# A two-layer graph attention kernel: the preparation of its first layer reordered, with projections in four column tiles, x loaded ahead of the stores, and the last targets spread by TensorE

## The chip, the cores and the metric

The kernel runs on one core of a Trainium2 chip. The core has five engines that work side by side, each through its own instructions in order: TensorE (PE, with its weight loads shown apart as PEld), VectorE (DVE), ScalarE (ACT), GpSimd (POOL) and SyncE (SP). SP issues all the transfers of this kernel; they then run on sixteen DMA engines. On-chip memory (SBUF) and the accumulators of TensorE (PSUM) have 128 partitions each. The metric is the device time of one execution in microseconds (us). "Before" took 4940.27 us, the median of three runs (4938.2 to 4942.55).

## What is computed

x is 4096 x 512, adj is 4096 x 4096, all in fp32. Each of two layers normalises x, applies a relu, and adds an attention over the graph with 8 heads of 64 columns. The change lies in the first layer alone:

```python
h = relu(layernorm(x))
data1 = (h @ W.T + b).reshape(N, 8, 64)
src = einsum('nhd,hd->nh', data1, src_proj)
trg = einsum('nhd,hd->nh', data1, trg_proj)
e = leaky(src.T[:, :, None] + trg.T[:, None, :])      # slope 0.01; [head, row, column]
scores = softmax(e + adj, axis=-1)
x = x + concat_over_heads(scores @ data1[head])
```

The second layer (projections to keys, queries and values, masked softmax, projection back) follows and is left as it is.

## The kernel before, in words

**The order** is written out by hand: inside `tc.manual_schedule()` the instructions stand on every engine in the order in which the Python code emits them. Pools of buffers and the dependencies between tiles add the waits. A tile of a pool with n buffers waits until the readers of the tile n allocations earlier are done. The transfers of SP use eight completion semaphores in turn, so a transfer also waits, on SP, for the one eight before it.

**The preparation of layer 0** works on eight blocks of 512 rows (`XR` = 4 tiles of 128 rows, `NQ` = 8). A loop over q (line 446) runs as a pipeline, each iteration doing another stage of several blocks:

- `load_rows` (310): a block of x, 1 MB, into one of the three buffers of pool `pa`. These three buffers later hold the rows of adj.
- `moments` (316) on VectorE, `deviations` (323) on ScalarE, `normed` (327): mean and variance, the square root, then reciprocal and shift on VectorE and the normalised rows `hn` on GpSimd.
- `turned_rows` (342): sixteen 128 x 128 transposes on TensorE (tile `htp`); ScalarE takes them with a relu into `hT`.
- `halves` (357): `lp` = `u`.T applied to `hT`, with the four row tiles of the block side by side in four column tiles of TensorE; VectorE adds the bias `cs` into `lr`. Each quarter of `lr` holds 8 source logits and 8 target logits for 128 rows. Four stores of 4 KB each write the target logits to `trg_d` in HBM.
- `sources` (373): `lr` turned by TensorE (tile `sp`), copied into `src` by VectorE.
- `first_features` (381): data1 for the first pair of heads (tile `mp`), two row tiles at a time; `first_features_out` (395) adds the bias on VectorE. After both halves of a block it also issues the store of that block's `hT`, 1 MB, to `hT_d`.

`u` holds W.T times the two projection vectors of each head, so that source and target logits come straight from `hT`. `prepared` (269), in iteration 1, makes it: VectorE spreads the projection vectors (`col`) into `by_head`, sixteen matmuls with W (`wn`) stationary give `up`, another sixteen give the bias, and VectorE copies both out. `turned_weights` (295) transposes W into `wt`.

**The targets** must stand on all 128 partitions, since the logits of 128 rows against 4096 columns are one ScalarE instruction: `leaky` (145), targets as the input, the row's source as a bias per partition. `load_targets` (123) reads `trg_d` back with a broadcast, in four parts of 1024 columns for each of the two heads, after every second block.

**The main loop** (474) then takes one head of a group of 128 rows at each step s: `leaky`, `masked` (152, VectorE adds a row of adj and takes the row's extreme, in two halves), `exps` (165, ScalarE), transposes on TensorE (`turned`, `taken`), and the product with the features (`weighted`). `hT_d` is read back here, for the features of the next pair of heads. The first three steps also work off what is left of the first features.

Of the kernel before, what the change touches and what calls it, by code (L numbers as in the profile page):

```python
# [8 lines left out]
F32 = mybir.dt.float32  # L9
AF = mybir.ActivationFunctionType  # L10
ALU = mybir.AluOpType
# [4 lines left out]
P = 128  # L16
EPS = 1e-5
SLOPE = 0.01
# [5 lines left out]
def kernel(  # L24
# [74 lines left out]
    with tc.tile_pool(name="a0k", bufs=1) as pk, tc.tile_pool(name="a0v", bufs=4) as pv, tc.tile_pool(  # L99
# [42 lines left out]
            nc.sync.dma_start(a, adj[bass.ts(G.g, P), bass.ts(f, CH)])  # L142
            rows_of_adj[G, f] = a

        def leaky(G, h):
            t = pt.tile([P, N], F32, name="t")
            nc.scalar.activation(  # L147
                t, targets[G.c, h], AF.Prelu, bias=src[:, G.g, 2 * G.c + h : 2 * G.c + h + 1], alpha=SLOPE
            )
            G.t[h] = t  # L150

        def masked(G, h, f):

# [98 lines left out]
        bb = pk.tile([P, HD], F32, name="bb")  # L252
        cs = pk.tile([P, 1], F32, name="cs")

        def load_wn():
            wn = []
            for i in range(2):
                wn.append(pv.tile([P, HC // 2, DM], F32, tag="v", name="wn"))
                nc.sync.dma_start(
                    wn[i], w0[bass.ts(i, HD // 2), :].rearrange("(c p) i -> p c i", p=P)  # L260
                )
            col = psb.tile([P, 3, HC], F32, name="col")
            for i, vec in enumerate(
                (src_proj.rearrange("x h d -> (x h d)"), trg_proj.rearrange("x h d -> (x h d)"), b0)
            ):
                nc.sync.dma_start(col[:, i], vec.rearrange("(c p) -> p c", p=P))
            return wn, col

        def prepared(wn, col):


            by_head = px.tile([P, HC, SQ], F32, tag="att", name="by_head")
            nc.vector.memset(by_head, 0.0)
            for c in range(HC):
                for half in range(2):
                    rows = bass.ts(half, D)
                    at = 2 * c + half
                    nc.vector.tensor_copy(by_head[rows, c, at : at + H + 1 : H], col[rows, 0:2, c])
            up = ptr.tile([P, TW], F32, tag="tr", name="up")
            for kc in range(KC):  # L280
                for c in range(HC):
                    nc.tensor.matmul(
                        up[:, bass.ts(kc, SQ)], lhsT=wn[c // 2][:, c % 2, bass.ts(kc, P)], rhs=by_head[:, c],
                        start=(c == 0), stop=(c == HC - 1),
                    )
            for j in range(NS):
                for c in range(HC):
                    nc.tensor.matmul(
                        up[bass.ts(j, SQ), 512:513], lhsT=by_head[:, c], rhs=col[:, 2, c : c + 1],
                        start=(c == 0), stop=(c == HC - 1),  # L290
                    )
            nc.vector.tensor_copy(u.rearrange("p c k -> p (c k)"), up[:, :P])
            nc.vector.tensor_copy(cs, up[:, 512:513])

        def turned_weights(wn):
            for j in range(KC // 2):
# [60 lines left out]
        def halves(R, q):  # L357

            lp = ptr.tile([P, TW], F32, tag="tr", name="lp")
            for kc in range(KC):  # L360
                for r in range(XR):
                    nc.tensor.matmul(
                        lp[bass.ts(r, SQ), :P], lhsT=u[:, kc], rhs=R.hT[:, r, kc, :],
                        start=(kc == 0), stop=(kc == KC - 1),
                    )
            R.lr = pp.tile([P, TW], F32, tag="pT", name="lr")[:, :P]
            nc.vector.tensor_scalar(R.lr, lp[:, :P], cs, None, ALU.add)
            for r in range(XR):
                nc.sync.dma_start(
                    trg_d[:, bass.ts(q * XR + r, P)], R.lr[r * SQ + H : r * SQ + 2 * H, :]  # L370
                )

        def sources(R, q):

# [20 lines left out]
        def first_features_out(q, j, tp):  # L395
            nc.vector.tensor_add(
                feats[0][q // 2][:, bass.ts(q % 2 * 2 + j, 2), :],
                tp[:, : 2 * PR].rearrange("p (r d) -> p r d", r=2),
                bb[:, :PR].unsqueeze(1).to_broadcast([P, 2, PR]),
            )  # L400
            if j == 1:
                nc.sync.dma_start(
                    hT_d[bass.ts(q, XR)].rearrange("r p k -> p r k"),
                    rows[q].hT.rearrange("p r k n -> p r (k n)"),
                )

        def sources_by_sets():

# [16 lines left out]
        def step(n):  # L425
            return groups[n // 2], n % 2

        with tc.manual_schedule():
            NQ = NB // XR
            TB = 8  # L430
            rows = [load_rows(0)]
            wn, col = load_wn()
            rows.append(load_rows(1))
            nc.sync.dma_start(bb, b0.partition_broadcast(P))
            todo = [(q, j) for q in range(NQ) for j in range(XR // 2)]
            made = []

            def some_features(ready):
                if todo and todo[0][0] < ready:
                    made.append(first_features(*todo.pop(0)))  # L440

            def some_out():
                if made:
                    first_features_out(*made.pop(0))

            for q in range(NQ + 4):
                if q + 2 < NQ:
                    rows.append(load_rows(q + 2))
                some_out()
                if 0 <= q - 2 < NQ:  # L450
                    turned_rows(rows[q - 2], q - 2)
                if 0 <= q - 1 < NQ:
                    normed(rows[q - 1])
                if q < NQ:
                    moments(rows[q])
                    deviations(rows[q])
                if q == 1:
                    prepared(wn, col)
                    turned_weights(wn)
                n = q - 3  # L460
                if 0 <= n < NQ:
                    halves(rows[n], n)
                    if (n + 1) * XR % TB == 0:
                        for h in range(2):
                            load_targets(0, h, n * XR // TB, NB // TB)
                if 0 <= n - 1 < NQ:
                    sources(rows[n - 1], n - 1)
                some_features(q - 2)
            some_out()
            for f in range(NCH):  # L470
                load_adj(groups[0], f)
            leaky(*step(0))
            endings = []
            for s in range(total + 6):
                G, h = step(s) if s < total else (None, 0)
                for half in range(2):

                    if s < total and half == h and s // 2 + 1 < len(groups):
                        load_adj(groups[s // 2 + 1], h)
                    n = 2 * s + half - LEAD  # L480
                    turn = 0 <= n < 2 * total
                    if turn:
                        T, i = groups[n // HALVES], n % HALVES
                        trs = turned(T, i)
                    if s < 3:
                        some_features(NQ)
                        some_features(NQ)
                    if (s, half) == (3, 1):
                        assert not todo and not made
                        sources_by_sets()  # L490
                    if half == 0 and 0 <= s - 1 < total:
                        exps(*step(s - 1))
                    if half == 1 and s + 1 < total:
                        leaky(*step(s + 1))

                        c, at = divmod(s + 3, 2 * NB)
                        if 0 < c < PAIRS and at < 2:
                            load_targets(c, at)
                    if s < total:
                        masked(G, h, half)  # L500
                    if s < 3:
                        some_out()
                        some_out()
                    for e in endings:
                        next(e, None)
                    if turn:
                        taken(T, i, trs)
                    if 1 <= n <= 2 * total:
                        W, w = groups[(n - 1) // HALVES], (n - 1) % HALVES
                        weighted(W, w)  # L510
                        if w == 0:
                            load_rows_turned(W)
                        if W.g == NB - 1 and W.c + 1 < PAIRS:
                            load_feats(W.c + 1, w)
                        if w == HALVES - 1:
                            endings = [*endings[-1:], finish(W)]
# [696 lines left out]
```

## Time and profile before

| What | Value |
|---|---|
| runs | 4938.2, 4940.27, 4942.55 us |
| the profiled execution | 4940.09 us |
| its span | 4938.3 us |
| TensorE busy | 4719.5 us, 96% |
| VectorE busy | 4462.5 us, 90% |
| ScalarE busy | 3857.6 us, 78% |
| GpSimd busy | 459.2 us, 9% |
| transfers | 819.44 MB, 166 GB/s over the span |
| first matmul | 17.08 us |
| first logits (`leaky`) | 88.30 us |
| first exponential (`exps`) | 102.37 us |

The span runs from the first to the last instruction of the profiled execution; the time of a run is a little longer. In the chain of waits each line gives a start, a duration and what the end of the kernel hung on at that moment: a transfer, an instruction of an engine, or the sequencer of one (SPq). In the timeline a line gives start, duration, engine, source line, operation, output, inputs, shapes and how many instructions it stands for. An fp32 matmul makes two passes in the records: 16 instructions are "x32". Idle time of an engine means nothing by itself; what counts is who waits for whom.

### The profile page before, as it was taken

What the parts mean: (1) busy time and instruction counts of PE and PEld (TensorE: products, weight loads), DVE (VectorE), ACT (ScalarE), POOL (GpSimd) and SP (SyncE); (2) the same over time, 40 slices, a digit from 0 to 9 for tenths busy, and PEclk for the clock granted to TensorE, in tenths of its full rate; (3) what the DMA queues carried; (4) which work ended last, traced back from release to release, by engine and by line L of the source; (5) the groups of instructions that cost most, each with busy time, mean ns of one, the idle gap of its engine ahead of it and who ended that gap; (6) DMA issues with size and microseconds to landing.
All of it is one profiled execution on the core that took longest, in us unless ns stands there. A gap on an engine that the chain in (4) does not pass through costs nothing.

```text
span 4938.3 us, 144474 instructions
## 1 busy us (share of the span) xinstructions
PE 4719.5 (96%) x61554; PEld 3518.5 (71%) x61554; DVE 4462.5 (90%) x7841; ACT 3857.6 (78%) x4301; POOL 459.2 (9%) x932
## 2 busy tenths in 40 slices
PE   6999999999999958989989999999999999999998
PEld 5888888888888847767756666666666666666664
DVE  4999999999999898888749999999999999999981
ACT  4999999999999899888748888766666666666660
POOL 2000000000000011111123333100000000000000
PEclk8999999999999979999999999999999999999999
DMA  6444454445444384444367787633445343534435
GB/s 233 158 152 157 162 193 161 152 153 206 153 156 158 115 181 135 143 140 135 111 192 249 241 265 237 223 130 131 152 152 170 130 156 129 189 129 136 158 124 192
DMA packets 358838, 819.44 MB, mean 166 GB/s; under 512 B 60080, under 2 KB 179120, under 8 KB 333104
## 3 DMA queue, kind: packets, MB, share of 16 engines
q1 hardware_dynamic: 358192, 810.21, 50.0%
q8 instruction: 481, 7.88, 0.6%
q14 instruction: 165, 1.35, 0.1%
HBM read 669.26 MB, written 140.77 MB: 164 GB/s over the span
## 4 chain that ended last, share of the span: by engine, by line
PE 57%; ACT 15%; DVE 15%; issue 8%; DMA 3%; SPq 1%; POOL 0%; DVEq 0%; ACTq 0%; POOLq 0%
PE sc L920 20%; PE o L1004 20%; ACT t L168 6%; PE tr L986 5%; DVE t L158 5%; DVE pT L192 4%; ACT t L147 4%; DVE bt L609 3%; PE tr L181 3%; PE o L203 3%; ACT pT L190 2%; PE oo L1087 2%; ACT bt L641 2%; DVE bt L648 2%; DMA ba<-in_adj_dram 1%
## 5 line engine op out<-in xcount | busy, mean ns | idle before, releaser
L936 DVE CUSTOM_DVE_ANT_0 t<-sc,a 128x512 f32<-128x512 f32 x2048 | 1285.7, 683 | 99.3 <-PE sc L920 52.0
L971 ACT ACTIVATE t<-t,nm 128x1024 f32<-128x1024 f32 x1024 | 1165.9, 1142 | 103.1 <-DVE nm L960 103.0
L1004 PEld LDWEIGHTS o<-t,v 128*64 128x64 f32 x16384 | 883.8, 137 | 429.4 <-issue 321.2
L920 PE MATMUL sc<-k,q 64*32 64x512 f32 x16384 | 1028.1, 597 | 10.5 <-DVE nm L936 10.4
L1004 PE MATMUL o<-t,v 128*64 128x128 f32 x16384 | 1007.4, 276 | 0.4 <-ACT oT L1013 0.4
L158 DVE CUSTOM_DVE_ANT_0 t<-t,a 128x2048 f32<-128x2048 f32 x384 | 876.0, 2281 | 41.2 <-ACT t L147 41.0
L978 DVE STREAM_TRANSPOSE t<-t 128x1536 f32<-128x1536 f32 x512 | 908.2, 1774 | 1.1 <-ACT t L971 1.1
L181 PE MATMUL tr<-ident,t 128*128 128x128 f32 x6144 | 781.5, 278 | 34.1 <-ACT pT L190 20.1
L203 PE MATMUL o<-pT,v 128*64 128x128 f32 x12288 | 756.8, 276 | 1.0 <-DVE pT L192 0.8
L181 PEld LDWEIGHTS tr<-ident,t 128*128 128x128 f32 x6144 | 665.4, 141 | 125.9 <-issue 65.3
L147 ACT ACTIVATE t<-tb,src 128x4096 f32<-128x4096 f32 x192 | 730.1, 3803 | 18.7 <-DMA tb<-trg_d 18.7
L168 ACT ACTIVATE t<-t,nm 128x4096 f32<-128x4096 f32 x192 | 729.8, 3801 | 8.5 <-DVE nm L163 8.4
L203 PEld LDWEIGHTS o<-pT,v 128*64 128x64 f32 x12288 | 664.0, 137 | 61.3 <-issue 46.8
L993 ACT COPY t<-tr 128x1024 f32<-128x1024 f32 x256 | 259.1, 1012 | 515.9 <-PE tr L986 507.0
L192 DVE COPY pT<-tr 128x1024 f32<-128x1024 f32 x549 | 652.5, 1213 | 9.8 <-PE tr L181 9.8
L920 PEld LDWEIGHTS sc<-k,q 64*32 64x32 f32 x16384 | 259.4, 106 | 371.8 <-issue 215.5
L599 ACT ACTIVATE lk<-tb,srcb 128x1024 f32<-128x1024 f32 x256 | 282.3, 1113 | 82.3 <-DVE nm L609 75.0
L609 DVE CUSTOM_DVE_ANT_0 bt<-lk,ba 128x1024 f32<-128x1024 f32 x256 | 302.0, 1215 | 24.8 <-ACT e L733 12.7
L648 DVE STREAM_TRANSPOSE bt<-bt 128x2048 f32<-128x2048 f32 x128 | 295.2, 2307 | 29.0 <-ACT bt L641 29.0
L641 ACT ACTIVATE bt<-bt,nm 128x1024 f32<-128x1024 f32 x256 | 290.3, 1135 | 0.4 <-DVE nm L630 0.3
L656 PE MATMUL bo<-bt,bv 128*64 128x128 f32 x4096 | 282.8, 297 | 5.9 <-ACT boT L665 4.5
L986 PE MATMUL tr<-ident,t 128*128 128x128 f32 x2048 | 280.8, 280 | 0.8 <-ACT t L971 0.7
(115 smaller groups left out, 3750.5 us busy)
## 6 DMA issues: line engine op xcount, KB each, us to landing
a<-in_adj_dram SPq DMA_DIRECT2D x192, 1024.0 KB
a<-pen_d SPq DMA_DIRECT2D x384, 512.0 KB
ba<-in_adj_dram SPq DMA_DIRECT2D x512, 128.0 KB
a<-in_adj_dram SPq DMA_DIRECT2D x512, 128.0 KB
pen_d<-a SPq DMA_DIRECT2D x128, 512.0 KB
h<-hT_d SPq DMA_DIRECT2D x96, 256.0 KB
qk_d<-e SPq DMA_DIRECT2D x64, 256.0 KB
x<-in_x_dram SPq DMA_DIRECT2D x8, 1024.0 KB
```

What stands on the lines that cost most here:

```text
L147: nc.scalar.activation(t, targets[G.c, h], AF.Prelu, bias=src[:, G.g, 2 * G.c + h : 2 * G.c + h + 1], alpha=SLOPE)
L158: nc.vector.tensor_tensor_reduce(out=t, in0=t, in1=rows_of_adj[G, f], scale=-1.0, scalar=FMAX, op0=ALU.add, op1=ALU.min, accum_out=nm[:, f ...
L168: nc.scalar.activation(G.t[h], G.t[h], AF.Exp, bias=G.nm[h][:, NCH : NCH + 1], scale=-1.0, accum_out=G.sm[:, h : h + 1],)
L181: nc.tensor.transpose(tr[:, bass.ts(b % 4 * 2 + h, P)], G.t[h][:, bass.ts(i * MB + b, P)], ident)
L192: nc.vector.tensor_copy(pT, tr)
L203: nc.tensor.matmul(G.o[h * D : (h + 1) * D, :P], lhsT=feats[G.c][i][:, b, bass.ts(h, D)], rhs=pT[:, bass.ts(b % 4 * 2 + h, P)], start=(mb ...
L920: nc.tensor.matmul(sc[h][bass.ts(a, SQ), :], lhsT=G.q[bass.ts(h, D), bass.ds(G.q0 + k * SQ, SQ)], rhs=keys[G.c][half][bass.ts(h, D), a, :] ...
L936: nc.vector.tensor_tensor_reduce(out=t[:, G.ring + k, h, cols], in0=scs[half][h], in1=a[:, cols], scale=1.0, scalar=FMAX, op0=ALU.add, op1 ...
L971: nc.scalar.activation(u, u, AF.Exp, bias=G.nm[k // 2][:, k % 2, h : h + 1], scale=-1.0, accum_out=G.sm[:, h, k : k + 1],)
L978: nc.vector.transpose(u, u)
L986: nc.tensor.transpose(tr[:, j, h, bass.ts(m, P)], t[:, G.ring + k - 1 + j, h, bass.ds(VC + m * P, P)], ident,)
L1004: nc.tensor.matmul(G.o[bass.ts(h, D), :P], lhsT=v[:, b, bass.ts(h, D)], rhs=t[:, bass.ds(G.ring, GS), h, bass.ds(at, SQ)], start=(mb == 0) ...
```

## The change

- **Projection of the weights.** `by_head`, 32 columns wide, becomes the stationary operand of `up` and W the moving one: four groups of columns of W go to four column tiles. The result stands the other way round, so ScalarE copies it (`uT`), TensorE turns it (`ut`) and ScalarE copies it into `u`. ScalarE also copies `cs`. `columns` and `prepared` move from iteration 1 to iteration 0, `turned_weights` from 1 to 2, behind the transposes of block 0.
- **Order of transfers.** The three small loads of `col` stand ahead of W; three blocks of x are loaded at the start. In the loop a block's projections (`halves`) come first in the iteration, then the next load of x, then the read-back of targets. The `hT` stores are separate (`stored`): two in iterations 7 and 8 of 0 to 10, six in the first three steps of the main loop. The first adj rows are loaded in iteration 9.
- **lr** is made by ScalarE, in buffers of pool `px`; `sources` follows in the same iteration, so the loop has one iteration fewer. First features start at iteration 4, and nine of the sixteen groups are left to the first steps, where seven were.
- **Last targets.** Blocks 6 and 7 are not read back. GpSimd makes a matrix of zeros and ones (`pick`) that selects one target row; TensorE multiplies it with `lr`, which puts that row on all partitions, and VectorE copies it into the targets.
- **First logits** in two instructions of 2048 columns.
- A one-element square root at the start loads ScalarE's table before data is there.

```diff
-        def leaky(G, h):
-            t = pt.tile([P, N], F32, name="t")
+        def leaky(G, h, part=0, parts=1):
+            if part == 0:
+                G.t[h] = pt.tile([P, N], F32, name="t")
+            cols = bass.ts(part, N // parts)
+            tpart = G.t[h][:, cols]
...
-            for kc in range(KC):
-                for c in range(HC):
+            for c in range(HC):
+                for kc in range(KC):
                     nc.tensor.matmul(
-                        up[:, bass.ts(kc, SQ)], lhsT=wn[c // 2][:, c % 2, bass.ts(kc, P)], rhs=by_head[:, c],
+                        up[bass.ts(kc, SQ), :P], lhsT=by_head[:, c], rhs=wn[c // 2][:, c % 2, bass.ts(kc, P)],
                         start=(c == 0), stop=(c == HC - 1),
                     )
+            uT = px.tile([P, P], F32, tag="xt", name="uT")
+            nc.scalar.copy(uT, up[:, :P])
...
-            nc.vector.tensor_copy(u.rearrange("p c k -> p (c k)"), up[:, :P])
-            nc.vector.tensor_copy(cs, up[:, 512:513])
+            nc.scalar.copy(cs, up[:, 512:513])
+            ut = po.tile([P, 4 * P], F32, tag="o", name="ut")
+            nc.tensor.transpose(ut[:, :P], uT, ident)
+            nc.scalar.copy(u.rearrange("p c k -> p (c k)"), ut[:, :P])
...
-            R.lr = pp.tile([P, TW], F32, tag="pT", name="lr")[:, :P]
-            nc.vector.tensor_scalar(R.lr, lp[:, :P], cs, None, ALU.add)
+            R.lr = px.tile([P, P], F32, tag=("att", "xt", "d1")[q % 3], name="lr")
+            nc.scalar.activation(R.lr, lp[:, :P], AF.Identity, bias=cs)
...
+        def picked():
+            pick = pp.tile([P, XR, 2, P], F32, tag="pT", name="pick")
+            for h in range(2):
+                nc.gpsimd.tensor_mul(
+                    pick[:, :, h],
+                    own.unsqueeze(2).to_broadcast([P, XR, P]),
+                    band[:, H + h : H + h + 1].unsqueeze(2).to_broadcast([P, XR, P]),
+                )
+            return pick
+
+        def targets_of(R, q, pick):
+            tp = ptr.tile([P, TW], F32, tag="tr", name="tgp")
+            for h in range(2):
+                for r in range(XR):
+                    nc.tensor.matmul(
+                        tp[:, bass.ts(h * XR + r, P)], lhsT=pick[:, r, h], rhs=R.lr, start=True, stop=True
+                    )
+            for h in range(2):
+                nc.vector.tensor_copy(targets[0, h][:, bass.ts(q, XR * P)], tp[:, bass.ts(h, XR * P)])
...
             rows = [load_rows(0)]
-            wn, col = load_wn()
+            col = load_col()
+            wn = load_wn()
             rows.append(load_rows(1))
+            rows.append(load_rows(2))
...
+            warm = psb.tile([P, 1], F32, name="warm")
+            nc.scalar.activation(warm, eps, AF.Sqrt)
...
-            for q in range(NQ + 4):
-                if q + 2 < NQ:
+            for q in range(NQ + 3):
+                n = q - 3
+                if 0 <= n < NQ:
+                    halves(rows[n], n)
+                    if n == NQ - 1:
+                        targets_of(rows[n - 1], n - 1, pick)
+                        targets_of(rows[n], n, pick)
+                if 3 <= q + 2 < NQ:
                     rows.append(load_rows(q + 2))
+                if n in (2, 4, 6):
+                    for h in range(2):
+                        cols = bass.ts(n // 2 - 1, 2 * XR * P)
+                        nc.sync.dma_start(targets[0, h][:, cols], trg_d[h, cols].partition_broadcast(P))
+                if q in (NQ - 1, NQ):
+                    stored(kept.pop(0))
+                if q == NQ + 1:
+                    for f in range(NCH):
+                        load_adj(groups[0], f)
+                if n == NQ - 1:
+                    leaky(*step(0), 0, 2)
+                    leaky(*step(0), 1, 2)
                 some_out()
...
-                if q == 1:
-                    prepared(wn, col)
+                if q == NQ:
+                    pick = picked()
...
+                if q == 0:
+                    by_head = columns(col)
+                    prepared(wn, col, by_head)
+                if q == 2:
                     turned_weights(wn)
-                n = q - 3
                 if 0 <= n < NQ:
-                    halves(rows[n], n)
-                    if (n + 1) * XR % TB == 0:
-                        for h in range(2):
-                            load_targets(0, h, n * XR // TB, NB // TB)
-                if 0 <= n - 1 < NQ:
-                    sources(rows[n - 1], n - 1)
-                some_features(q - 2)
-            some_out()
-            for f in range(NCH):
-                load_adj(groups[0], f)
-            leaky(*step(0))
+                    sources(rows[n], n)
+                if q > 3:
+                    some_features(q - 2)
...
                     if s < 3:
                         some_features(NQ)
                         some_features(NQ)
+                        if kept:
+                            stored(kept.pop(0))
```

More of the change, by code (lines that the diff above doesn't have):

```diff
@@ L143, in load_adj @@
             rows_of_adj[G, f] = a
-        def leaky(G, h):
-            t = pt.tile([P, N], F32, name="t")
+        def leaky(G, h, part=0, parts=1):
[3 more added lines that the diff above has]
+            tpart = G.t[h][:, cols]
             nc.scalar.activation(
-                t, targets[G.c, h], AF.Prelu, bias=src[:, G.g, 2 * G.c + h : 2 * G.c + h + 1], alpha=SLOPE
+                tpart, targets[G.c, h][:, cols], AF.Prelu, bias=src[:, G.g, 2 * G.c + h : 2 * G.c + h + 1],
+                alpha=SLOPE,
             )
-            G.t[h] = t
         def masked(G, h, f):
@@ L253, with load_col @@
         cs = pk.tile([P, 1], F32, name="cs")
+        def load_col():
+            col = psb.tile([P, 3, HC], F32, name="col")
+            for i, vec in enumerate(
+                (src_proj.rearrange("x h d -> (x h d)"), trg_proj.rearrange("x h d -> (x h d)"), b0)
+            ):
+                nc.sync.dma_start(col[:, i], vec.rearrange("(c p) -> p c", p=P))
+            return col
         def load_wn():
@@ L261, in load_wn, with columns @@
                 )
[L262 to L269, printed above, removed]
+            return wn
+        def columns(col):
             by_head = px.tile([P, HC, SQ], F32, tag="att", name="by_head")
@@ L278, in prepared @@
                     nc.vector.tensor_copy(by_head[rows, c, at : at + H + 1 : H], col[rows, 0:2, c])
+            return by_head
+        def prepared(wn, col, by_head):
             up = ptr.tile([P, TW], F32, tag="tr", name="up")
-            for kc in range(KC):
-                for c in range(HC):
+            for c in range(HC):
+                for kc in range(KC):
                     nc.tensor.matmul(
-                        up[:, bass.ts(kc, SQ)], lhsT=wn[c // 2][:, c % 2, bass.ts(kc, P)], rhs=by_head[:, c],
+                        up[bass.ts(kc, SQ), :P], lhsT=by_head[:, c], rhs=wn[c // 2][:, c % 2, bass.ts(kc, P)],
                         start=(c == 0), stop=(c == HC - 1),
                     )
+            uT = px.tile([P, P], F32, tag="xt", name="uT")
+            nc.scalar.copy(uT, up[:, :P])
             for j in range(NS):
@@ L400, in first_features_out, with stored @@
             )
[L401 to L405, printed above, removed]
+        def stored(q):
+            nc.sync.dma_start(
+                hT_d[bass.ts(q, XR)].rearrange("r p k -> p r k"),
+                rows[q].hT.rearrange("p r k n -> p r (k n)"),
+            )
         def sources_by_sets():
@@ L429 @@
             NQ = NB // XR
-            TB = 8
             rows = [load_rows(0)]
-            wn, col = load_wn()
+            col = load_col()
+            wn = load_wn()
             rows.append(load_rows(1))
+            rows.append(load_rows(2))
             nc.sync.dma_start(bb, b0.partition_broadcast(P))
+            for h in range(2):
+                targets[0, h] = pk.tile([P, N], F32, tag=f"tb{h}", name=f"tb{h}")
+            warm = psb.tile([P, 1], F32, name="warm")
+            nc.scalar.activation(warm, eps, AF.Sqrt)
             todo = [(q, j) for q in range(NQ) for j in range(XR // 2)]
             made = []
+            kept = list(range(NQ))
             def some_features(ready):
@@ L444, in some_out @@
                     first_features_out(*made.pop(0))
-            for q in range(NQ + 4):
-                if q + 2 < NQ:
-                    rows.append(load_rows(q + 2))
+            for q in range(NQ + 3):
[6 more added lines that the diff above has]
+                if 3 <= q + 2 < NQ:
+                    rows.append(load_rows(q + 2))
+                if n in (2, 4, 6):
+                    for h in range(2):
+                        cols = bass.ts(n // 2 - 1, 2 * XR * P)
[8 more added lines that the diff above has]
+                    leaky(*step(0), 1, 2)
                 some_out()
@@ L487 @@
                         some_features(NQ)
+                        if kept:
+                            stored(kept.pop(0))
                     if (s, half) == (3, 1):
-                        assert not todo and not made
+                        assert not todo and not made and not kept
                         sources_by_sets()
```

## The prediction

> **What bounds the kernel now.** I read the page first: TensorE is busy 96% and VectorE 90% of a 4938.3 us span, but these are averages over stages that the change does not touch. The diff lies in the preparation of layer 0, so I went to the chain of waits in order of time, up to 100 us:
>
> ```profile
> 36.32 5.79 DMA x<-in_x_dram
> ...
> 42.43 5.24 DMA trg_d<-lr
> ...
> 48.73 8.69 DMA x<-in_x_dram
> ...
> 62.05 9.53 DMA hT_d<-hT
> 71.60 1.21 DMA trg_d<-lr
> ...
> 73.39 6.30 DMA tb<-trg_d
> 79.71 3.64 DMA trg_d<-lr
> ...
> 83.99 4.21 DMA tb<-trg_d
> ...
> 91.91 3.70 ACT t L147
> 95.63 2.29 DVE t L158
> ```
>
> From 36 to 88 us the chain is almost all transfers, one after the other: a block of x, the small stores of the logits (trg_d), a store of hT, the read-back of the logits on all partitions (tb). The engines run in bursts between them. The timeline of the same stretch gives durations and order:
>
> ```profile
> 16.68 1.46 DVE L278 COPY by_head<-col 64x2 f32<-64x2 f32 x8
> 17.08 7.04 PE L282 MATMUL up<-by_head,wn 128*128 128x32 f32 x32 [17.08 <-DVE by_head L278]
> 24.04 1.31 PE L288 MATMUL up<-col,by_head 128*32 128x1 f32 x32
> 25.28 3.67 PE L300 MATMUL wtp<-ident,wn 128*128 128x128 f32 x16
> ...
> 37.73 1.08 PE L362 MATMUL lp<-hT,u 128*32 128x128 f32 x32
> 38.90 1.95 PE L387 MATMUL mp<-wt,hT 128*128 128x128 f32 x16
> 40.69 1.91 PE L350 MATMUL htp<-ident,hn 128*128 128x128 f32 x16
> 42.53 1.08 PE L362 MATMUL lp<-hT,u 128*32 128x128 f32 x32
> ...
> 75.31 7.26 SPq L369 DMA_DIRECT2D trg_d<-lr  x8
> ...
> 88.30 7.31 ACT L147 ACTIVATE t<-tb,src 128x4096 f32<-128x4096 f32 x2 [18.66 <-DMA tb<-trg_d]
> 95.63 2.29 DVE L158 CUSTOM_DVE_ANT_0 t<-t,a 128x2048 f32<-128x2048 f32 x1 [18.62 <-ACT t L147]
> ...
> 102.37 3.71 ACT L168 ACTIVATE t<-t,nm 128x4096 f32<-128x4096 f32 x1
> ```
>
> Three readings. The first matrix product of the preparation waits until 17.08 us, since its operand stands on VectorE behind the second block's statistics. Where data is there (37.73 to 42.53), one block takes 4.80 us, and TensorE is continuous in it (1.08 + 0.16 + 1.95 + 1.91, overlapping a little): TensorE sets that pace. The main loop gets going with its first exponential at 102.37 us. From there ScalarE alternates logits and exponentials of 3.7 us each. So what moves 102.37 moves the end by as much, unless it is given back.
>
> **What the skill says.** The Trainium skill, "TensorE: Matmul & The Clock Gate", Part 1, has a cold array at half rate until about 3.4 us of sustained work. The trace agrees in size: 16 transposes take 3.67 us at 25.28 and 1.91 us later; the fast rate came some 4.9 us into them. Part 4 of that page says that transposes don't count as work for the clock; here they evidently did. "TensorEngine Tiling (Array Packing)", When to Use Tiling, gives four column tiles for a stationary operand 32 wide: agreed, lp makes 32 passes in 1.08 us, mp 16 in 1.95. "DMA: Bandwidth & Descriptors", Anatomy of one DMA, prices a transfer at 2.0 us plus bytes over 436 GB/s, an estimate of 4.4 us for 1 MB; the trace has 5.8 for x at 36.32, and that is used. "ScalarE: Activation LUTs", What ACT_TABLE_LOAD costs, says 1283 ns; the trace shows 1.28.
>
> **The change, step by step.** I rebuild the start from the new order on each engine. Blocks are 0 to 7; iteration q turns block q-2 and projects block q-3.
> 1. The first x lands at 6.3 as before (it has less beside it; perhaps 0.9 earlier, not counted). Statistics and three constants until 9.9, then by_head at once: 0.17 + 1.46, 11.7. Moved in SP's queue: the three loads of col (issue 0.92, 0.53, 1.76) now stand ahead of the two of W (wn, 0.46 each), whose issue slips from 1.2 to about 4.5. W is still ahead of the second x, which landed at 13.19 before, so it comes between 9 and 13; I take it as there by 11.7, at worst 1.3 later. The third x now goes out beside them, not behind bb.
> 2. up, now by_head stationary in four tiles: 32 passes, nearest row lp while slow, 1.54 (bounds 1.08 and the old 7.04): 13.2. Copy on ScalarE: no row of 128 columns; between 0.30 (rstd) and 1.01 (1024 columns), I take 0.4: 13.7. The bias product, which waits for that copy, 1.31: 15.0. Turning u back, 0.33: 15.4. The table load of 1.28 on rstd is now under the first transfer.
> 3. htp(0), slow: 3.7, 19.1 (hn(0) is there from GpSimd at 15.2). The weights' turn, moved behind it: about four slow and twelve fast, 2.3: 21.4. lp(0) 1.08, htp(1) 1.91: 24.4. lp(1) waits for ScalarE's second half of hT(1), 1.2: 25.6.
> 4. Six iterations at 4.80: 54.4. Cover: VectorE needs 4.2 in each (statistics 3.2, src 0.18, v 0.42, reciprocal and shift 0.4), GpSimd 3.03, ScalarE 2.7 with lr (moved from VectorE, 0.4). An x load waits until GpSimd has normed the block three earlier, whose buffer it takes. That ends 3.9 into an iteration (v and two small operations 0.8, then 3.03); the statistics want the block two iterations on, at 0.9: 6.6 us, against 0.1 and the 5.8 measured. This cover is thin, 0.7; another 1.7 lies between GpSimd's end and the turn on TensorE. In SP's queue an x load now stands behind the four logit stores of its iteration (1.40 to 1.88 us to issue), which are ready before GpSimd frees the buffer, but ahead of the read-backs and of every hT store.
>    New waits here: the turn of lr (sp) needs ScalarE's lr of the same iteration, 0.4 long, with 1.91 of htp between. From block 3 on lr's buffer waits on ScalarE for the stores of the lr three blocks (14.4 us) back; the chain shows 5.24 for such stores. If they were late, the two hT copies queued behind lr, and with them TensorE, would be late too. The issues of these stores wait on SP only for transfers eight back, the hT store of block 0 among them for block 6; behind them is the last read-back.
> 5. lp(7) 1.08, 55.5. Targets of blocks 6 and 7: 16 matmuls, two mp groups of 1.95: 59.4. Four copies of 512 columns at about 0.65 (half of the 1024-column copy, 1.21): the one that half the first logits wait for ends at 60.1, the last at 60.7. This replaces store, wait and read-back (lr at 72.73 to the landing at 88.20, 15.5 us).
> 6. Logits, part one: only the read-backs of blocks 0 to 3, landed before 50; about 1.9 for 2048 columns (half of 3.70), done by 58. Part two, 60.1 to 62.0. Its other input, the read-back of blocks 4 and 5, is issued near 53 and lands near 57.5.
> 7. VectorE after the copies: v 0.42, src 0.18, mask one at 61.3 to 63.6; two v, 0.84; mask two 64.5 to 66.8; minimum 0.25; table load 1.28. First exponential at 68.3.
>
> 102.37 - 68.3 = 34.1 us earlier. Costed at nothing: six of eight hT stores move into the first three steps of the loop. Each is 2.6 us of the engines at the 400 GB/s that full stretches show, 15.7 in all; the adjacency loads beside them are needed a step (7.4 us) apart, and hT is read back only about 20 us later. Uncovered they would cost 15.7. Nine groups of first features instead of seven run in those steps: 2 x 1.95 on TensorE and 2 x 0.42 on VectorE, under ScalarE's 7.4 a step.
>
> Against the profiled execution, 4940.09 (span 4938.3 and 1.8 around it; median of the runs 4940.27): 4940.1 - 34.1 = 4906.0.
>
> **Rivals.**
> A, TensorE-paced as above: 4906, own range 4900 to 4914 (up at its bounds -0.5 and +5.5, three copies on ScalarE up to +1.8, the targets' products at the slow clock +3.5, the earlier x -0.9, a longer fast stretch -3).
> B, transfers pace it: x, read-backs and stores share the engines and a block takes 6 to 6.5 us. For: before, x took 8.69 us at 48.73 with hT and tb beside it. Against: the last x is now issued ahead of these. Six blocks at +1.5: 9 us, 4915.
> C, the hT stores collide with the adjacency loads and the whole 15.7 comes back: 4922. Against: the order puts only one pair of loads behind them, with ten us to spare.
> D, the other side: the array stays at half rate. Place: iterations 2 to 10 and the features after them. htp 3.67, mp 3.7, lp 1.54, sp 0.3 make 9.2 a block, 4.4 more; six blocks 26, the start 4, the targets 4, the features that VectorE waits for some 10: 44, so 10 slower than before, 4950. For: the array was slow from 17 to 30 us though busy. Against: it turned fast after 4.9 and, at 61 to 64, after 2.9 us of dense work, and there is no pause of that length ahead. It decides if the slow rate lasts about eight of the blocks.
> E, most of the gain does not arrive: the first masks wait for the first adjacency rows, which now stand on SP behind block 6's stores and the last read-back. It ends within 0.2% if they land 25 us later than the 60 to 63 that 3 MB ahead of them at 0.4 MB a microsecond give from 53.
>
> **How the numbers follow.** A 0.70, B 0.16, C 0.06, D 0.03, E 0.05. The prediction is A's. A, B and C are all faster by more than 0.2% (9.9 us, about what a measurement of this kernel can tell): 0.92. E is the 0.05 within, D the 0.03 slower. The range takes A's own, with 2 us below it for what I called uncounted, and reaches up over B to C's middle: 4898 to 4922, which leaves out D, E and half of C, with the edges of A about 0.15.
>
> **What would show it.** Right: up near 1.5 us and started by 12; eight lp groups spaced 4.8 us with VectorE not waiting for x by more than 1 us; tgp near 56; first exponential at 65 to 72; the loop's spacing unchanged behind it. Wrong: lp spacing of 6 or more with waits for x (B); masks of the first steps waiting for a (C); htp groups still at 3.7 us beyond 25 us (D).

## The result and the profile after

The changed kernel takes 4909.15 us (median; 4906.02 to 4909.64), against 4939.24 us for the kernel before, measured beside it: a ratio of 0.9937, with a 95% interval of 0.992 to 0.9954. That is 30 us faster. The forecast was 4906, range 4898 to 4922. The profiled execution took 4906.02 us with a span of 4904.2, so the spans of the two profiled executions differ by 34.1 us, which is what the sum had.

The chain of waits of the changed kernel, in order of time (start, duration, what the end hung on):

```profile
20.72 1.01 PE lp L375 x32
...
44.06 1.05 PE lp L375 x32
...
48.90 4.03 DMA trg_d<-lr
...
53.01 0.35 SPq L501
...
53.93 8.99 DMA a<-in_adj_dram
...
63.06 2.29 DVE t L161
```

From 10.5 to 45 us the chain is TensorE with short pieces of ScalarE; the transfers that filled it from 36 us on are gone. But it doesn't stay on TensorE to the end of the preparation. From 48.90 it runs through a small store of block 5, the last read-back (L501 is its issue), and the first rows of adj.

The timeline of the changed kernel:

```profile
10.48 1.94 PE L291 MATMUL up<-wn,by_head 128*32 128x128 f32 x32 [10.48 <-DVE by_head L283]
...
20.65 1.08 PE L375 MATMUL lp<-hT,u 128*32 128x128 f32 x32
...
48.79 1.08 PE L375 MATMUL lp<-hT,u 128*32 128x128 f32 x32
...
53.60 1.08 PE L375 MATMUL lp<-hT,u 128*32 128x128 f32 x32
54.61 3.84 PE L402 MATMUL tgp<-lr,pick 128*128 128x128 f32 x32
...
59.21 5.60 ACT L150 ACTIVATE t<-tb,src 128x2048 f32<-128x2048 f32 x2 [2.16 <-DVE tb L406]
...
63.06 2.29 DVE L161 CUSTOM_DVE_ANT_0 t<-t,a 128x2048 f32<-128x2048 f32 x1 [2.86 <-DMA a<-in_adj_dram]
64.83 1.28 ACT L171 ACT_TABLE_LOAD   x1
...
68.46 3.71 ACT L171 ACTIVATE t<-t,nm 128x4096 f32<-128x4096 f32 x1 [2.35 <-DVE nm L166]
```

The first exponential starts at 68.46 instead of 102.37, 33.91 us earlier. Where they come from:

| Stretch | before | after | gained |
|---|---|---|---|
| start to the first `lp` | 32.99 | 20.65 | 12.34 |
| first `lp` to the last | 38.54 | 32.95 | 5.59 |
| last `lp` to the first exponential | 30.84 | 14.86 | 15.98 |

The lines of the kernel before that this rests on, beside its exponential at 102.37:

```profile
32.99 1.08 PE L362 MATMUL lp<-hT,u 128*32 128x128 f32 x32
...
57.45 0.69 DVE L320 BATCH_NORM_STATS2 stats<-x 128x6 f32<-128x512 f32 x1 [6.24 <-DMA x<-in_x_dram]
...
71.53 1.08 PE L362 MATMUL lp<-hT,u 128*32 128x128 f32 x32
```

The start wins what the operand and the order save, the middle loses the pause for the last x (57.45), the end loses a read-back. The rest keeps the gain: the last exponential of the first main loop starts at 1664.3 instead of 1698.7 us, 34.4 earlier.

The untouched stages vary by a few us between executions. From the last exponential of the first main loop to the last one of the loop after it (the last pair of heads) there are 746.0 us before, 746.4 after, and 749.7 in experiment 5 below, which differs only ahead of them. The first main loop itself is steadier: from its first exponential to its last there are 1595.4 to 1596.9 us in ten of the twelve traces (the exceptions are experiments 8 and 9). So the experiments are read by the first exponential of their trace (for short: **first exp**), with the times beside it. The groups of experiments were timed on different chips, each beside the kernel before, so between groups the ratios compare, and not the microseconds.

### The profile page after: what moved, and what is told of

Same layout as the page of the kernel before. It is cut to its first block, busy times and chain, and to the rows that moved or that the text cites. A ratio compares the mean times of both kernels' runs of the same rounds, so it can differ in the third digit from the quotient of the medians.

```text
span 4904.2 us, 144545 instructions
## 1 busy us (share of the span) xinstructions
PE 4716.6 (96%) x61587; PEld 3515.3 (72%) x61587; DVE 4462.8 (91%) x7835; ACT 3861.6 (79%) x4314; POOL 462.9 (9%) x934
## 4 chain that ended last, share of the span: by engine, by line
PE 56%; ACT 16%; DVE 16%; issue 8%; DMA 3%; SPq 1%; DVEq 0%; POOL 0%; ACTq 0%; POOLq 0%
PE o L1062 20%; PE sc L978 20%; ACT t L171 6%; DVE t L161 6%; PE tr L1044 5%; DVE pT L195 4%; ACT t L150 4%; DVE bt L667 3%; ACT pT L193 2%; PE oo L1145 2%; ACT bt L699 2%; PE tr L184 2%; PE o L206 2%; DVE bt L706 2%; DMA ba<-in_adj_dram 1%
## 5 line engine op out<-in xcount | busy, mean ns | idle before, releaser
L978 PE MATMUL sc<-k,q 64*32 64x512 f32 x16384 | 1028.4, 597 | 10.4 <-DVE nm L994 10.3
L150 ACT ACTIVATE t<-tb,src 128x4096 f32<-128x4096 f32 (+1 forms) x193 | 735.2, 3810 | 2.2 <-DVE tb L406 2.2
L667 DVE CUSTOM_DVE_ANT_0 bt<-lk,ba 128x1024 f32<-128x1024 f32 x256 | 302.0, 1216 | 25.0 <-ACT e L791 11.1
```

The costliest lines, as they stand in the source:

```text
L150: nc.scalar.activation(tpart, targets[G.c, h][:, cols], AF.Prelu, bias=src[:, G.g, 2 * G.c + h : 2 * G.c + h + 1], alpha=SLOPE,)
L978: nc.tensor.matmul(sc[h][bass.ts(a, SQ), :], lhsT=G.q[bass.ts(h, D), bass.ds(G.q0 + k * SQ, SQ)], rhs=keys[G.c][half][bass.ts(h, D), a, :] ...
```

## The experiments

Each edit is to the changed kernel, unless it says otherwise.

**1. The old start** (`e1_old_start`). Do the gains add up along one chain, or do stores and read-backs run on their own clock?

```diff
-                if q == 0:
+                if q == 1:
                     by_head = columns(col)
                     prepared(wn, col, by_head)
-                if q == 2:
                     turned_weights(wn)
...
+            nc.vector.tensor_copy(u.rearrange("p c k -> p (c k)"), up[:, :P])
+            nc.vector.tensor_copy(cs, up[:, 512:513])
...
+            wn = load_wn()
             col = load_col()
-            wn = load_wn()
...
-            warm = psb.tile([P, 1], F32, name="warm")
-            nc.scalar.activation(warm, eps, AF.Sqrt)
```

The matmuls of `up`, left out here, have W stationary again.

> The changed kernel with the start as before: W stationary, made in iteration 1, copied by VectorE, W loaded ahead of col, no early table load. Own theory (the preparation is one chain paced by TensorE, so its three gains add up): the first lp group falls back from 20.65 to 31 to 33 us, the last one and the first exponential move by the same 10 to 12 us, to 79 to 81; the kernel is 10 to 12 us slower than the changed one. Rival (the late part is bound by stores and read-backs on their own clock, so an earlier start is swallowed by them): first exponential at 72 or earlier, under 4 us slower.

4921.37 us (4917.26 to 4924.89), 0.9956 of the kernel before (0.9941 to 0.997). Timeline:

```profile
16.74 7.03 PE L291 MATMUL up<-by_head,wn 128*128 128x32 f32 x32 [16.74 <-DVE by_head L283]
...
31.73 1.07 PE L371 MATMUL lp<-hT,u 128*32 128x128 f32 x28 [0.50 <-ACT hT L362]
...
64.66 1.08 PE L371 MATMUL lp<-hT,u 128*32 128x128 f32 x32
...
79.94 3.71 ACT L171 ACTIVATE t<-t,nm 128x4096 f32<-128x4096 f32 x1 [2.76 <-DVE nm L166]
```

Last `lp` 11.06 later (64.66 against 53.60), first exp 11.48 later: everything behind the start moves with it, the wait for the rows of adj too (3.27 us here, 2.86 in the changed kernel). Against the kernel before measured beside it this version is 20 us faster, where the changed kernel is 30 faster; the intervals of the two ratios overlap a little, so the trace is the better witness. The theory of one chain holds, the rival falls.

**2. The new start alone, on the kernel before** (`e2_start_only`): `columns` and `prepared` of the change, in iteration 0, `col` ahead of W, three blocks of x at once, the early table load.

```diff
+                if q == 0:
+                    by_head = columns(col)
+                    prepared(wn, col, by_head)
-                if q == 1:
-                    prepared(wn, col)
+                if q == 2:
                     turned_weights(wn)
```

> The kernel before with the new start alone (operand swapped, iteration 0, three blocks of x at once, early table load). Own theory: the chain of transfers of before begins with an x load that waits for GpSimd, so it begins earlier by what the start gives; first exponential at 90 to 93 instead of 102.37, 10 to 12 us faster than before. Rival (transfers on their own clock): under 4 us faster.

4930.92 us (4927.51 to 4934.44), ratio 0.9978 (0.9969 to 0.9986). Timeline:

```profile
22.04 1.08 PE L372 MATMUL lp<-hT,u 128*32 128x128 f32 x32
...
92.95 3.71 ACT L168 ACTIVATE t<-t,nm 128x4096 f32<-128x4096 f32 x1
```

First exp comes 9.42 earlier than before; the time says about 11. The first `lp` came 10.95 earlier, so 1.5 us were lost on the way: here the first mask waited for the first rows of adj until 86.22. With experiment 1 this shows that the start carries 9 to 12 us with the old stages behind it and with the new ones.

**3. The last targets read back** (`e3_read_back`):

```diff
-                        targets_of(rows[n - 1], n - 1, pick)
-                        targets_of(rows[n], n, pick)
+                        for h in range(2):
+                            cols = bass.ts(3, 2 * XR * P)
+                            nc.sync.dma_start(targets[0, h][:, cols], trg_d[h, cols].partition_broadcast(P))
```

> The changed kernel with the targets of blocks 6 and 7 read back from HBM instead of made by TensorE. Own theory: the small stores are issued near 56, land near 62 behind the adjacency rows, the read-back lands near 67; second half of the first logits at 67 to 69 instead of 59.2, first exponential at 73 to 76, 5 to 8 us slower than the changed kernel. Rival (the whole 15.5 us that the read-back took before come back): first exponential at 83 or later. Second rival (the adjacency rows end the wait anyway): no more than 2 us slower.

4917.91 us (4916.86 to 4920.19), ratio 0.995 (0.9935 to 0.9964); first exp at 78.30, 9.84 later. My interval, 73 to 76, was missed, and so were both rivals'. Timeline:

```profile
57.40 1.52 SPq L382 DMA_DIRECT2D trg_d<-lr  x4
67.13 0.88 SPq L495 DMA_DIRECT2D tb<-trg_d  x2
...
70.92 2.00 ACT L150 ACTIVATE t<-tb,src 128x2048 f32<-128x2048 f32 x1 [13.62 <-DMA tb<-trg_d]
```

The four stores of 4 KB are issued by 58.9, and the read-back can go out at 67.13 only: SP waited 7.5 us in one piece for a store to land, behind a read-back and two rows of adj. From `lr` (made by 55.4) to the second half of the logits are 15.5 us; in the kernel before there were 15.2 (from 73.1 to 88.30). With TensorE it is 4.05 (from 55.16 to 59.21). So the replaced link is worth 11.5 us, and 9.84 arrive, since the rows of adj would have held the start anyway.

**4. The last x behind a read-back and a store** (`e4_x_behind`). In the kernel before only the read-back stood ahead of this load, and the store just behind it (the load was issued at 48.73, the store at 49.25), so this puts one transfer more ahead of x than the kernel before had:

```diff
+                if n in (2, 4, 6):
+                    ...
+                if q == 5:
+                    stored(kept.pop(0))
                 if 3 <= q + 2 < NQ:
                     rows.append(load_rows(q + 2))
-                if n in (2, 4, 6):
-                    ...
```

> The changed kernel with the last load of x (block 7) behind the first read-back of targets and behind the store of hT of block 0, as it stood in the kernel before. Own theory: the pace is TensorE's and the last x has some slack; x lands 2 to 4 us later, the last lp group moves by 0 to 1.5 us. Rival (the order of x and stores is what the change won in the loop): the last lp group and the first exponential come 5 us or more later, as before, where this x took 8.69 us.

4911.64 us (4908.48 to 4914.1), ratio 0.9938 (0.9921 to 0.9955). Timeline:

```profile
43.73 1.08 PE L375 MATMUL lp<-hT,u 128*32 128x128 f32 x32
...
44.39 0.69 DVE L333 BATCH_NORM_STATS2 stats<-x 128x6 f32<-128x512 f32 x1 [4.64 <-DMA x<-in_x_dram]
...
49.54 3.58 PE L422 MATMUL mp<-wt,hT 128*128 128x128 f32 x16
...
53.05 1.08 PE L375 MATMUL lp<-hT,u 128*32 128x128 f32 x32
```

I expected 0 to 1.5 us. The load, issued at nearly the same moment (34.10 against 33.71), lands at 44.39, while in the changed kernel VectorE took this x at 39.91 without waiting. One `lp` gap grows from 4.8 to 9.3, and the last `lp` is 4.25 late (57.85). Not all of that is waiting: TensorE stood still for 2.7 us, since ScalarE waited for the moments of the late block (until 47.78) with its work for the block before queued behind; and soon after the pause the features (`mp`) took 3.58 us instead of 1.95, with a recorded clock of 0.50. The rival's size, 5 or more, isn't reached, but its mechanism is at work: the place of the last x in the queue is worth microseconds, and not fractions of one. How much of the 5.59 us that the middle gained is due to it stays open, since the order of the kernel before was not put back exactly: there the load took 8.69 us, and SP came to it only at 48.73, when GpSimd had been done with its buffer since 46.07. First exp is 2.99 late (71.45): the wait for adj at the end, 1.60 here instead of 2.86, took up the rest. The time is no witness here: its ratio is that of the changed kernel.

**5. Rows of adj earlier, no store of hT in the loop** (`e5_adj_early`):

```diff
-                if q in (NQ - 1, NQ):
-                    stored(kept.pop(0))
-                if q == NQ + 1:
+                if q == NQ:
                     for f in range(NCH):
                         load_adj(groups[0], f)
...
-                        if kept:
-                            stored(kept.pop(0))
+                        for _ in range(1 + (s > 0 and half == 0)):
+                            if kept:
+                                stored(kept.pop(0))
```

> The changed kernel with the first two adjacency rows loaded one iteration earlier and no store of hT in the loop (all eight in the first three steps). Theory from the trace of the changed kernel: its first mask waits for the adjacency rows (63.06, when logits and copies were ready at about 60.2), because the small stores of block 5 and the last read-back wait behind stores of hT. Expected: first mask at 60 to 61, first exponential at 66 to 67 instead of 68.46, 1.5 to 2.5 us faster, too little for the timed runs. Rival (the eight stores of hT crowd the first steps): later masks wait for adjacency rows and the third exponential is no earlier than in the changed kernel.

4906.39 us (4905.82 to 4907.99), ratio 0.9929 (0.9915 to 0.9942). Timeline:

```profile
59.82 2.28 DVE L161 CUSTOM_DVE_ANT_0 t<-t,a 128x2048 f32<-128x2048 f32 x1
...
64.53 1.28 ACT L171 ACT_TABLE_LOAD   x1
65.83 3.71 ACT L171 ACTIVATE t<-t,nm 128x4096 f32<-128x4096 f32 x1
...
78.32 2.29 DVE L161 CUSTOM_DVE_ANT_0 t<-t,a 128x2048 f32<-128x2048 f32 x1 [1.74 <-DMA a<-in_adj_dram]
```

The first mask no longer waits, first exp comes 2.63 earlier (0.30 of it was there at the last `lp` already), and ScalarE is continuous from logits over table load to exponential. A later mask waits 1.74 us for its rows, and 0.47 of the gain is lost by the third exponential, which is still 2.16 earlier (80.91 against 83.07). So the adjacency rows did end the preparation of the changed kernel, and eight stores in the first steps cost half a microsecond. The edit does two things at once, and which of them brought the rows forward isn't separated.

**6. The first logits in one piece** (`e6_one_piece`):

```diff
-                    leaky(*step(0), 0, 2)
-                    leaky(*step(0), 1, 2)
+                    leaky(*step(0))
```

> The changed kernel with the first logits in one instruction of 4096 columns. Theory: the split buys nothing, since the first mask waits for adjacency rows until 63.06 and the first exponential for the second mask; the one piece runs from 59.2 to 62.9, the second head's logits end near 66.6, the table load after them near 67.9; first exponential at 68 to 69, within 0.7 us of 68.46. Rival: the split is worth its 1.9 us.

One execution, 4912.65 us; first exp at 70.46, 2.0 later. My "within 0.7" was wrong. The rival's number, 1.9, came true, but not through the split itself. Timeline:

```profile
69.17 1.28 ACT L171 ACT_TABLE_LOAD   x1 [3.17 <-DVE nm L166]
```

The first mask was late by 0.67 only, through rows that landed later; their loads stand ahead of the edit in the program, so this part may be chance. The other 1.28 is the table load: here it stands behind the wait for the minimum, as in the kernel before; in the changed kernel it ran at 64.83, ahead of that wait. All twelve traces fall in line: with the logits in two pieces the load starts as soon as the logits are done (eight traces), and with one piece it waits for the minimum (four traces). In these four a separate semaphore instruction stands just ahead of the load (139 of them belong to this line, 138 in the others). Why the program places it there no run shows.

**7. The same on the version of experiment 5** (`e10_early_one_piece`), one execution:

> The version with early adjacency rows, with the first logits in one instruction. In the changed kernel the one piece cost 2.0 us: 0.67 for rows that landed later, and 1.28 because the load of the exponential's table then stands behind the wait for the minimum. Theory: with the rows early the first mask also waits for the whole piece; first mask at 62.6 to 63, second at 65.8 to 66.3, table load behind the minimum again, first exponential at 69.3 to 70, 3.5 to 4.2 us later than 65.83. Rival (only the table load counts): 1.3 us later, at 67.1.

4910.03 us; first exp at 70.27, 4.44 later than 65.83 and a little beyond the 69.3 to 70 expected. In this run the logits began 0.89 later (59.80), so 3.55 belong to the edit, within the 3.5 to 4.2 expected. With the rows there in time, the first mask waits for the whole piece (63.54), and the table load stands behind the minimum as well. The split was worth more than the changed kernel could show.

**8. No first features in the loop** (`e7_no_features`), three groups to each half step behind it, one execution:

```diff
-                if q > 3:
-                    some_features(q - 2)
```

> The changed kernel with no first features inside the preparation loop; all sixteen groups are made in the first three steps, three to a half step. Own theory (TensorE sets the pace of 4.80 us): without the 1.95 us of features the lp groups stand 4.2 to 4.6 us apart, held by VectorE or the x loads; the last lp group comes 1.2 to 3.6 us earlier. It is given back in the steps, where VectorE then waits for features: the second exponential comes later than in the changed kernel. Rival (x loads set the pace anyway): the spacing stays at 4.7 to 4.8.

4915.29 us. Timeline:

```profile
45.65 1.07 PE L375 MATMUL lp<-hT,u 128*32 128x128 f32 x28 [0.50 <-ACT hT L366]
...
49.77 1.07 PE L375 MATMUL lp<-hT,u 128*32 128x128 f32 x28 [0.50 <-ACT hT L366]
...
79.73 3.71 ACT L171 ACTIVATE t<-t,nm 128x4096 f32<-128x4096 f32 x1 [5.12 <-DVE nm L166]
```

A block now takes 4.12 us, so TensorE did set the pace of 4.80, and x loads hold 4.12 as well. What sets 4.12 is neither VectorE nor x: `lp` waits for ScalarE's second half of `hT`, that is, for transposes and copy one after the other. The last `lp` ends 3.84 earlier (50.84 against 54.68), a little more than the 3.6 I gave it. First exp gains 1.25 of that (67.21), and all is lost later: the second exponential starts at 79.73 instead of 75.77, the third 7.4 later, and the last one of this loop still 7.7 later.

**9. The old operand in the new place** (`e8_old_operand`): W stationary, VectorE copying, still in iteration 0; one execution.

```diff
-            for c in range(HC):
-                for kc in range(KC):
+            for kc in range(KC):
+                for c in range(HC):
                     nc.tensor.matmul(
-                        up[bass.ts(kc, SQ), :P], lhsT=by_head[:, c], rhs=wn[c // 2][:, c % 2, bass.ts(kc, P)],
+                        up[:, bass.ts(kc, SQ)], lhsT=wn[c // 2][:, c % 2, bass.ts(kc, P)], rhs=by_head[:, c],
```

> The changed kernel with W stationary in the first projection and VectorE copying it out, but still in iteration 0 and with all else changed. Own theory: the sixteen matmuls take about 7.0 us again instead of 1.94 and the turn back of u (about 1.0) goes, and VectorE's copy stands ahead of its next work; the first lp group comes 4 to 6 us later, at 25 to 27, and the first exponential by as much. Rival (only the place in the order counted, the operand hardly): under 2 us.

4917.68 us. Timeline:

```profile
10.90 7.04 PE L291 MATMUL up<-by_head,wn 128*128 128x32 f32 x32 [10.90 <-DVE by_head L283]
...
20.91 3.67 PE L359 MATMUL htp<-ident,hn 128*128 128x128 f32 x16 [1.73 <-POOL hn L347]
...
26.49 1.08 PE L371 MATMUL lp<-hT,u 128*32 128x128 f32 x32
```

The matmuls take 5.1 us more, and the first `lp` is 5.84 late: VectorE, which waits for them to copy `u`, comes late to the operands of `hn`, and TensorE waits another 1.73 for GpSimd. First exp at 76.41 is 7.95 late, beyond my 4 to 6: 6.81 were there at the last `lp` (60.41), and the first mask then waited longer for its rows. Of what experiment 1 took away, the operand (with its copies on ScalarE) is about half at the first `lp` (5.84 of 11.1) and two thirds at first exp (7.95 of 11.48); place and order are the rest.

**10. Fewer first features in the loop, rows of adj early** (`e11_fewer_features`), on the version of experiment 5:

```diff
-                if q > 3:
+                if q > 5:
                     some_features(q - 2)
```

> The version with early adjacency rows (first exponential 65.83), and first features in the loop only from iteration 6 on: five groups there, eleven in the first steps. The run without features in the loop showed a block in 4.12 us instead of 4.80, and gave it back because three groups stood in each half step. Theory: two iterations at 0.68 less, first exponential at 64.2 to 64.9; two groups to a half step (3.9 us of TensorE against 3.7 of ScalarE) give back up to 1 us by the third exponential, at 79.6 to 80.9 instead of 80.91. Rival: all of it is given back, third exponential at 81 or later.

4903.75 us (4902.91 to 4904.55), ratio 0.9926 (0.9913 to 0.994). Timeline:

```profile
64.34 3.71 ACT L171 ACTIVATE t<-t,nm 128x4096 f32<-128x4096 f32 x1
```

First exp comes 1.49 earlier than in experiment 5, the third exponential 1.96 earlier (78.95): nothing is given back. The traces put this version 4.12 ahead of the changed kernel at first exp, and 3.7 at the last exponential of the loop. The times agree in direction but don't prove it, since the intervals of the two ratios overlap. A version that starts the features one iteration later still (`e9_few_features`) gave no result: by my count of the code it has thirteen groups to write out in the first three steps, which have room for twelve.

## Why the prediction was right, and where its steps were off

**The mechanism and the sum.** That the preparation is one chain up to the first exponential, and that what is gained there reaches the end, is shown by experiments 1 to 3 in both directions, and by the steady main loop behind it. First exp was worked out as 68.3 and came at 68.46. Some of that agreement is luck, as the steps show.

**Steps 1 to 3, the start.** The first `lp` was put at 21.4; it began at 20.65. `up` started at 10.48, not 11.7, since its first matmul needs two of the eight copies of `by_head` and not all. It took 1.94 us, within the bounds of 1.08 to 7.04, above the 1.54 taken. Turning the weights took 3.00 us, not 2.3: with 0.229 us a transpose slow and 0.119 fast (3.67 and 1.91 over 16), about ten of sixteen were slow. W was there in time.

**Step 4, the middle.** Six iterations at 4.80 came true to the hundredth (24.78 to 53.60 is 28.82, six times 4.80), and experiment 8 shows that it was TensorE. The working named the cover of an x load as thin, 0.7 us and another 1.7, and that was right: VectorE waited 0.50 us for one block of the steady stretch (35.69), with no effect on TensorE. What was wrong is the weight that I gave it later, 0 to 1.5 us for an x behind other transfers; experiment 4 measures 4.25. There an x load with 2 MB issued just ahead of it took 10.3 us, not 5.8, and TensorE ran slow for a while behind the pause.

**Step 5, the targets.** Two groups in 3.84 us (3.9 said) and copies of 0.65. In experiment 3 the replaced link comes back with 15.5 us. My estimate of 5 to 8 for that experiment took the 4 KB stores to land within some 6 us; they took 8.

**Steps 6 and 7, the end.** Here the working named the wrong last wait. It had the first mask at 61.3 from VectorE's copies, with the rows of adj between 60 and 63; they landed at 62.9 and released it. The small stores of block 5 were issued by 48.9, behind a read-back (42.83) and a store of hT (43.69), and landed at 52.9; the last read-back waited for them, and the rows stood behind that on SP. It is rival E's mechanism, at 2.9 us of waiting instead of 25. Against it, the table load of 1.28, put behind the minimum, ran before it. The errors cancel: VectorE was ready for the first mask 1.1 us earlier than worked out, waited 2.9, then needed 0.3 less up to the second mask and 1.3 less up to the exponential. What is left is 0.16.

**Costed at nothing.** The six hT stores and nine groups of features in the first steps cost nothing that the trace shows: behind the first mask none in these steps waits for rows of adj in the changed kernel, and the first main loop takes 1595.8 us from first to last exponential, against 1596.3 before. With eight stores (experiment 5) one wait of 1.74 costs 0.47. Features are free at two to a half step (experiment 10) and not at three (experiment 8).

**The rivals.** B's mechanism exists (experiment 4), but needs x behind other transfers, and in the changed kernel it is ahead of them. C and D did not happen: the array was at full rate before the first `lp`. The time lies 3 us above the forecast, while the profiled execution is on it; that is within what the untouched stages vary, and its cause was not looked for.

**The clock and the table load.** The Trainium skill, "TensorE: Matmul & The Clock Gate", Part 4, says that transposes don't bring the fast clock. Here they did, or at least did not keep it away: from 14.3 to about 20 us TensorE did nothing but transposes, and in that stretch a transpose went from 0.229 to 0.119 us. The skill's 1283 ns for a table load ("ScalarE: Activation LUTs", What ACT_TABLE_LOAD costs) agrees with the 1.28 us in every trace; the question was only what the load stood behind.

## What to carry to other kernels

When a start-up phase is a chain of short stages, find the one instruction where the steady loop begins, work out when it comes, and follow every queue up to it: what moves it moves the end. What was issued just ahead of a transfer belongs to its price (5.8 us for 1 MB with little beside it, 10.3 with 2 MB ahead), so a load with a thin cover goes out before the bulk stores, and a small store whose read-back is awaited must not stand behind them. Once one wait is removed, look for the next to end last before counting the gain of a further step; the split of the first logits was worth 1.3 to 2.0 us with the rows late and about 3.5 with the rows in time.

## What the runs showed of the hardware

- Stores of 4 KB each, issued by 58.9 us while a read-back and two 1 MB loads were under way, let the next read-back out at 67.13 only (experiment 3).
- After a pause of 2.7 us of TensorE, eight transposes still ran fast (1.06 us), and the product behind them took 3.58 us instead of 1.95, with a recorded clock of 0.50 (experiment 4).
- The same product of the same operands took 7.04 us with the 128-wide operand stationary and the 32-wide moving, and 1.94 us the other way round in four column tiles, both with the array at the slow rate (the sixteen transposes behind them took 3.67 and 3.62 us, where they take 1.91 to 1.97 later).
- The load of an activation table (1.28 us) ran ahead of the wait for the minimum in the changed kernel and behind it in experiment 6; first exp was at 68.46 and 70.46, and 1.28 of the difference is this.
